# One value product for two heads on 64x64 tiles, and score products with 60 key columns

## The chip, the cores and the metric

The kernel runs on one core of one Trainium2 chip. The metric is the device time of one execution in microseconds. TensorE is called PE here, its weight loads PEld, VectorE DVE, ScalarE ACT, GpSimd POOL and SyncE SP.

## The reference

One layer, on x of shape (2, 128, 256, 256) in float32: halo attention, then a mixture of experts on each pixel, both with a residual. Cut to what matters here:

```
x  = x + conv(layernorm_over_channels(x))
#   conv: qkv = W_qkv x (1x1); windows of 8x8 queries, 12x12 keys and values around them,
#   4 heads of 32 channels; logits = q k / sqrt(32) + relative position (height and width)
#   + a fixed mask that leaves the keys of the query's own parity;
#   softmax, times v, heads joined, W_out
t  = pixels of x as rows of 128 channels
p  = softmax(layernorm(t) @ router_w + router_b)        # 8 experts
t  = t + sum over the two best experts of (weight * (layernorm(t) @ expert_w[e] + expert_b[e]))
```

The mask splits the image into four planes by the parity of row and column; within a plane a window has 4x4 queries and 6x6 keys.

## The kernel before

The image is cut into 64 strips of 8 rows (2 images of 32 strips), each strip into its 4 parity planes: 256 *planes*, each a turn of the main loop over `n` (line 811). A plane has 4 x 128 = 512 queries, that is 16 pairs of windows; the pairs are in two `half`s of 8, counted by `t`. A pair of windows shares `NK` = 6 x 10 = 60 keys; they lie in slots of `SLOT` = 64, so that two halves fill 128 partitions. Keys 60 to 63 of a slot are zero.

On PE a plane has these stages, always in this order:

- `scores`: 16 products of `keys` with `au` (L476), which lay the position terms and the mask into `att[:, :, 0:256]`, one PSUM bank for each head; then 64 products of the keys `kk` with the queries `qs` (L493), one for each `t`, head and half, which add to them. ACT takes the exponential of all into `pT` (L501).
- `project` of the next plane: values `pv` (L349, 4 products), position terms `pu` (L408), keys `pk` (L422), queries `pq` (L447).
- four expert products (L716) of an earlier plane.
- `attend`: 8 products with `ones` (L514), which lay the softmax sums into banks 2 and 3 of `att`, columns 256 to 511; then 64 products of the values `vv` with `pT` (L524), one for each `t`, half and head, into the same columns of banks 0 and 1. DVE transposes the sums (`sT`, L534), takes the reciprocals (`rc`, L536), transposes them back (`rT`, L539) and multiplies (`o`, L544).
- `norms` (L582, 16 products), three expert products (L716), `po` from `o` (L552), one expert product (L716).

DVE makes the other products of the expert part: the gated inputs `xe` of each expert (L707), the sums of the experts (L722), the routing (L615 to L653), and the relative position terms (`uT`, `auT`, `au`: L412 to L396). SP issues nearly all DMAs, in the order of the program. For some of them another engine first writes one element of the tile that is to be loaded, so that the load is placed in time: the copies L688 and L114 on ACT, the memset L690 on DVE.

The order of all engines' instructions is written out by hand in the main loop, under `manual_schedule`; nothing reorders them. From plane 6 on, a plane begins with

```
            if 6 <= n < n_planes:
                nc.tensor.addr_align(BLOCK, offset=BLOCK - FIRST_LIMIT)
```

which puts no-ops into PE's program until the address of the next instruction, counted in instructions, is `BLOCK - FIRST_LIMIT` modulo `BLOCK`. A float32 product is four PE instructions: two times a weight load and a pass.

## Time and profile before

| | us |
|---|---|
| three timed runs | 4332.03, 4342.97, 4343.37 (median 4342.97) |
| the profiled execution | 4328.49 |
| its span, from the first to the last instruction | 4326.7 |

| engine | busy us | share of the span |
|---|---|---|
| PE passes | 4223.3 | 98% |
| PE weight loads | 2472.0 | 57% |
| DVE | 3791.0 | 88% |
| ACT | 1320.7 | 31% |
| POOL | 1087.6 | 25% |

The DMA queue that SP feeds takes 75.9% of the time of the 16 DMA engines; queue q8, which brings PE's program, 1.2%. The granted clock of PE is 0.991 on average.

How to read the lines: a group's line gives line, engine and operation, output <- inputs by the program's names, tile of the array (rows*columns), shapes, and the count; behind the bar the busy time in us and the mean of one in ns; then the idle time of the engine ahead of it, and what ended most of it. "issue" is a wait for nothing that the profile shows. A timeline's line gives start and length in us; consecutive instructions of one kind stand as one, and a length can reach over the next one's start, since the ends of PE's passes are modelled.

### The profile page before, as it was taken

What the parts mean: (1) busy time and instruction counts of PE and PEld (TensorE: products, weight loads), DVE (VectorE), ACT (ScalarE), POOL (GpSimd) and SP (SyncE); (2) the same over time, 40 slices, a digit from 0 to 9 for tenths busy, and PEclk for the clock granted to TensorE, in tenths of its full rate; (3) what the DMA queues carried; (4) which work ended last, traced back from release to release, by engine and by line L of the source; (5) the groups of instructions that cost most, each with busy time, mean ns of one, the idle gap of its engine ahead of it and who ended that gap; (6) DMA issues with size and microseconds to landing.
All of it is one profiled execution on the core that took longest, in us unless ns stands there. A gap on an engine that the chain in (4) does not pass through costs nothing. (4 is left out here: it accounts for less than half of the span.)

```text
span 4326.7 us, 224393 instructions
## 1 busy us (share of the span) xinstructions
PE 4223.3 (98%) x94273; PEld 2472.0 (57%) x94273; DVE 3791.0 (88%) x11850; ACT 1320.7 (31%) x3774; POOL 1087.6 (25%) x1126
## 2 busy tenths in 40 slices
PE   7899999999999999999999999999999999999987
PEld 5455555555555555555555555555555555555553
DVE  5788988988888889988888998898998889899877
ACT  3233332332323232333333233233332333333321
POOL 1222222222222222222222222222222222222211
PEclk8999999999999999999999999999999999999999
DMA  3777778787788778777778778778788787787866
GB/s 109 214 234 247 241 244 244 244 247 235 244 236 242 240 243 248 239 246 239 247 237 247 248 240 247 239 244 250 239 248 244 239 249 237 248 243 244 243 191 193
DMA packets 824578, 1022.17 MB, mean 236 GB/s; under 512 B 137634, under 2 KB 409634, under 8 KB 823594
## 3 DMA queue, kind: packets, MB, share of 16 engines
q1 hardware_dynamic: 822864, 1007.52, 75.9%
q8 instruction: 769, 12.60, 1.2%
q14 instruction: 215, 1.76, 0.1%
q10 hardware_dynamic: 730, 0.29, 0.0%
HBM read 863.78 MB, written 143.75 MB: 233 GB/s over the span
## 5 line engine op out<-in xcount | busy, mean ns | idle before, releaser
L716 PE MATMUL acc<-xe,ew 128*128 128x512 f32 x4096 | 1917.9, 601 | 18.6 <-DVE gb L690 14.3
L716 PEld LDWEIGHTS acc<-xe,ew 128*128 128x128 f32 x4096 | 758.4, 190 | 939.7 <-issue 873.1
L707 DVE TENSOR_TENSOR xe<-xs,gb 128x512 f32<-128x512 f32 x1536 | 950.8, 687 | 11.6 <-DMA gb<-gd 1.5
L711 POOL COPY last<-xe 128x1 f32<-128x1 f32 x256 | 47.6, 186 | 3115.3 <-DVE gb L690 3082.2
L707 POOL TENSOR_TENSOR xe<-xs,gb 128x512 f32<-128x512 f32 x512 | 652.3, 1275 | 1.5 <-PE att L524 1.2
L493 PE MATMUL att<-qs,kcol 32*64 32x32 f32 x32768 | 402.1, 227 | 15.8 <-issue 15.4
L493 PEld LDWEIGHTS att<-qs,kcol 32*64 32x64 f32 x32768 | 397.5, 132 | 19.6 <-issue 18.9
L275 POOL TENSOR_TENSOR xn<-xt,rb 128x512 f32<-128x512 f32 x249 | 374.3, 1503 | 94.6 <-DMA rb<-gd 94.0
L524 PEld LDWEIGHTS att<-pT,vwin 64*32 64x32 f32 x32768 | 349.4, 105 | 42.0 <-issue 4.5
L501 ACT ACTIVATE pT<-att 128x1024 f32<-128x1024 f32 x256 | 262.2, 1024 | 298.8 <-PE att L493 298.8
L524 PE MATMUL att<-pT,vwin 64*32 64x32 f32 x32768 | 346.7, 200 | 2.7 <-issue 1.5
L349 PE MATMUL pv<-wt,xn 128*128 128x128 f32 x2048 | 303.8, 292 | 0.6 <-issue 0.6
L412 DVE STREAM_TRANSPOSE uT<-pu 128x512 f32<-128x512 f32 x256 | 183.6, 717 | 134.9 <-PE pu L408 134.9
L576 ACT ACTIVATE sq<-xt 128x512 f32<-128x512 f32 x505 | 292.6, 630 | 0.0
L396 DVE STREAM_TRANSPOSE au<-auT 128x512 f32<-128x512 f32 x256 | 269.6, 1053 | 9.0
L552 PE MATMUL po<-o,wt 128*128 128x512 f32 x512 | 263.6, 596 | 10.2 <-DVE o L544 6.6
L433 ACT COPY kcol<-pk 128x560 f32<-128x560 f32 (+2 forms) x344 | 183.5, 533 | 275.0 <-PE pk L422 272.2
L408 PE MATMUL pu<-xn,wrel 128*128 128x512 f32 x512 | 267.2, 604 | 0.0
L447 PE MATMUL pq<-xn,wt 128*128 128x512 f32 x512 | 262.1, 592 | 1.7 <-issue 1.7
L422 PE MATMUL pk<-xn,wt 128*128 128x512 f32 (+2 forms) x528 | 261.5, 579 | 0.0
L349 PEld LDWEIGHTS pv<-wt,xn 128*128 128x128 f32 x2048 | 254.1, 195 | 11.5 <-issue 1.0
L476 PEld LDWEIGHTS att<-au,keys 32*64 32x64 f32 x8192 | 117.6, 132 | 228.2 <-PE po L552 183.8
(2437 smaller groups left out, 4856.6 us busy)
## 6 DMA issues: line engine op xcount, KB each, us to landing
gb<-gd SPq DMA_DIRECT2D x2048, 256.0 KB, 5.6
vwin<-vrows SPq DMA_DIRECT2D x512, 240.0 KB, 5.1
xt<-in_x_dram SPq DMA_DIRECT2D x256, 256.0 KB, 6.6
sb<-gd SPq DMA_DIRECT2D x256, 256.0 KB, 4.4
out_dram<-xt SPq DMA_DIRECT2D x256, 256.0 KB, 6.0
rb<-gd SPq DMA_DIRECT2D x249, 256.0 KB, 3.4
vrows<-vr SPq DMA_DIRECT2D x168, 256.0 KB, 3.8
vrows<-vr SPq DMA_DIRECT2D x160, 128.0 KB, 3.6
```

The source lines that it names most:

```text
L275: eng.tensor_tensor(xn[i % 2][:, :, :, k, 1 : PC + 1], ln1_src(i, k).rearrange("p (y j x) -> p y x j", y=2, x=2), rb.rearrange("p (y j x) ...
L349: nc.tensor.matmul(pv[:, j * P : (j + 1) * P], lhsT=xp[:, k, 1 : PC + 1], rhs=wv, start=True, stop=True,)
L396: nc.vector.transpose(au.rearrange("p m a s -> p a s m"), auT[n % 2])
L408: nc.tensor.matmul(pu, lhsT=wrel, rhs=inner, start=True, stop=True)
L447: nc.tensor.matmul(pq, lhsT=wq, rhs=inner, start=True, stop=True)
L493: nc.tensor.matmul(sc[rows, h, 32 * t : 32 * t + 32], lhsT=kk[hp, half * HP + t, :], rhs=qs[hp, m0 : m0 + 2].rearrange("p m a s -> p (m a ...
L501: nc.scalar.activation(pT, att[:, :, 0:HQ], AF.Exp)
L524: nc.tensor.matmul(av[hp, half, 32 * t : 32 * t + 32], lhsT=vv[rows, t, hp], rhs=pT[rows, h, 32 * t : 32 * t + 32], start=True, stop=True,)
L552: nc.tensor.matmul(po, lhsT=wo, rhs=state["o"].rearrange("p f z -> p (f z)"), start=True, stop=True)
L576: nc.scalar.activation(sq, src, AF.Square)
L707: eng.tensor_tensor(self.xe[e], self.xs, self.gb.pop(e), ALU.mult)
L716: nc.tensor.matmul(self.acc, lhsT=ew[:, e, :], rhs=self.xe.pop(e), start=(e == 0), stop=not self.xe)
```

## The change

- The value products: one product takes 64 value channels, those of two heads, and the `pT` of both heads for one `t` and half, 64 columns side by side. It is 64 x 64 on 64 rows: 32 products in place of 64. Half of what it makes is of use (a head's channels with its own `pT`); the other half is left lying. The results fill all 512 columns of banks 0 and 1, where the scores were; `own` is the view of them by `t`, head of the pair `j` and query.
- The softmax sums stay where they were; `av` now names those two banks alone.
- For heads 1 and 3 ACT copies the half of use over the other within PSUM, two copies of 32 partitions, so that `o` can be made by one instruction from `own[:, :, :, 0]`.
- The score products take 60 key columns, not the 64 of a slot, and write 60 partitions.
- The no-ops align a plane to 128 instructions, 88 ahead of a multiple of 128; it was 256, and 99 ahead of a multiple of 256.

```diff
-BLOCK, FIRST_LIMIT = 256, 99
+BLOCK, FIRST_LIMIT = 128, 88
...
-                    rows = slice(half * SLOT, (half + 1) * SLOT)
+                    rows = slice(half * SLOT, half * SLOT + NK)
                     m0 = 2 * (half * HP + t)
                     nc.tensor.matmul(
                         sc[rows, h, 32 * t : 32 * t + 32],
-                        lhsT=kk[hp, half * HP + t, :],
+                        lhsT=kk[hp, half * HP + t, 0:NK],
                         rhs=qs[hp, m0 : m0 + 2].rearrange("p m a s -> p (m a s)"),
...
-        av = att[:, :, HQ:512]
+        av = att[:, 2:4, HQ:512]
+        own = att[:, 0:2].rearrange("p f (t j z) -> p f t j z", j=2, z=32)
...
-                    av[hp, 2 + half], lhsT=ones[rows, :], rhs=pT[rows, h], start=True, stop=True
+                    av[hp, half], lhsT=ones[rows, :], rhs=pT[rows, h], start=True, stop=True
...
-                for h in range(HEADS):
-                    hp = slice(h * DH, (h + 1) * DH)
+                for g in range(2):
+                    gp = slice(2 * g * DH, 2 * (g + 1) * DH)
                     nc.tensor.matmul(
-                        av[hp, half, 32 * t : 32 * t + 32],
-                        lhsT=vv[rows, t, hp],
-                        rhs=pT[rows, h, 32 * t : 32 * t + 32],
+                        att[gp, half, 64 * t : 64 * t + 64],
+                        lhsT=vv[rows, t, gp],
+                        rhs=pT[rows, 2 * g : 2 * g + 2, 32 * t : 32 * t + 32],
...
-        nc.vector.transpose(sT, av[:, 2:4])
+        nc.vector.transpose(sT, av)
         rc = small.tile([P, NQ // 32], F32, tag="rc", name=f"rc{n}")
         nc.vector.reciprocal(rc, sT.rearrange("p f (b k) -> p (f b) k", k=32)[:, :, 0])
+        for h in (1, 3):
+            hp = slice(h * DH, (h + 1) * DH)
+            nc.scalar.copy(own[hp, :, :, 0], own[hp, :, :, 1])
         yield
...
-        nc.vector.tensor_tensor(o, av[:, 0:2], rT, ALU.mult)
+        nc.vector.tensor_tensor(
+            o.rearrange("p f (t z) -> p f t z", z=32),
+            own[:, :, :, 0],
+            rT.rearrange("p f (t z) -> p f t z", z=32),
+            ALU.mult,
+        )
```

## The prediction

> **What bounds the kernel now.** First the page: the busy shares, the costliest groups, the DMA queues.

> ```profile
> PE 4223.3 (98%) x94273; PEld 2472.0 (57%) x94273; DVE 3791.0 (88%) x11850; ACT 1320.7 (31%) x3774; POOL 1087.6 (25%) x1126
> ...
> L493 PE MATMUL att<-qs,kcol 32*64 32x32 f32 x32768 | 402.1, 227 | 15.8 <-issue 15.4
> L493 PEld LDWEIGHTS att<-qs,kcol 32*64 32x64 f32 x32768 | 397.5, 132 | 19.6 <-issue 18.9
> ...
> L524 PEld LDWEIGHTS att<-pT,vwin 64*32 64x32 f32 x32768 | 349.4, 105 | 42.0 <-issue 4.5
> ...
> L524 PE MATMUL att<-pT,vwin 64*32 64x32 f32 x32768 | 346.7, 200 | 2.7 <-issue 1.5
> ...
> q8 instruction: 769, 12.60, 1.2%
> ```

> PE is solid. A product leaves four records (two weight loads, two passes), so a plane has 184 products, 736 PE instructions. With one wait and 31 no-ops (L825) that is 768; queue q8 moved 769 packets of 16,384 bytes, three a plane: one packet holds 256 instructions.

> The timeline of PE next: an undisturbed plane, then three disturbed ones.

> ```profile
> 246.94 0.69 PE L476 MATMUL att<-au,keys 32*64 32x128 f32 x32
> 247.43 1.53 PE L493 MATMUL att<-qs,kcol 32*64 32x32 f32 x128
> 248.88 1.16 PE L349 MATMUL pv<-wt,xn 128*128 128x128 f32 x8
> 249.88 1.02 PE L408 MATMUL pu<-xn,wrel 128*128 128x512 f32 x2
> 250.74 1.02 PE L422 MATMUL pk<-xn,wt 128*128 128x512 f32 x2
> 251.60 1.02 PE L447 MATMUL pq<-xn,wt 128*128 128x512 f32 x2
> 252.46 3.59 PE L716 MATMUL acc<-xe,ew 128*128 128x512 f32 x8
> 255.98 0.66 PE L514 MATMUL att<-pT,ones 64*32 64x256 f32 x16
> 256.44 1.34 PE L524 MATMUL att<-pT,vwin 64*32 64x32 f32 x128
> ```

> ```profile
> 211.33 0.37 PE L493 MATMUL att<-qs,kcol 32*64 32x32 f32 x17
> 213.57 1.22 PE L493 MATMUL att<-qs,kcol 32*64 32x32 f32 x90 [1.87 <-issue]
> ```

> ```profile
> 1088.48 1.45 PE L716 MATMUL acc<-xe,ew 128*128 128x512 f32 x3
> 1090.64 2.31 PE L716 MATMUL acc<-xe,ew 128*128 128x512 f32 x5 [0.71 <-issue]
> ```

> ```profile
> 2674.22 1.15 PE L524 MATMUL att<-pT,vwin 64*32 64x32 f32 x107
> 2675.69 0.32 PE L524 MATMUL att<-pT,vwin 64*32 64x32 f32 x21 [0.31 <-issue]
> ```

> The typical plane repeats in 16.268 us. The breaks stand after 17 score passes, 3 expert passes and 107 value passes: by count, instructions 99, 355 and 611 of the plane, the borders of the 256-instruction blocks, as 256 - 157 = 99 says. Over 239 middle planes the score, value and first expert stages lie 22.4, 6.5 and 6.0 us above their medians: 35 us lost at borders.

> The DMA packet records of queue q8, each with start and duration, say what PE waits for. Wherever PE breaks at a border, it resumes 1.42 us (1.23 to 1.62) after the end of the latest packet, and each border has its own: the packet whose transfer begins some 2.9 us after border 99 was passed is the one border 355 waits for, and so on. So one block is fetched ahead, and passing a border orders the next. In the 197 planes without a score break that packet ends on average 4.62 us after the plane's first product (5th to 95th percentile 3.73 to 5.65); the block is usable at 4.62 + 1.42 = 6.04 us. Border 355 lies at the second expert product, due at 5.52 + 3 x 0.43 = 6.81 us, which mostly hides it.

> **Borders (BLOCK, FIRST_LIMIT).** 32 products fewer are 128 instructions fewer: 608 products' instructions, two waits (a new one stands ahead of L476), 30 no-ops, 640 a plane, 2.5 blocks. Planes alternate: A has borders at 88, 344 and 600, B at 216 and 472. Counting A: the new wait 1, keys to 65, scores to 321, pv to 337, pu to 341, then pk's load, pass, load make 344: the border falls before pk's second pass, due 0.43 us after pk's start at 3.80, so at 4.23 us. The block behind it is ordered at 88, 11 instructions (0.05 us) before today's 99, so usable at 5.99 us. PE stands 5.99 - 4.23 = 1.76 us in every A plane; even the earliest of those packets would be late. pq, the expert products and all behind stand in PE's order behind pk, so nothing takes it back. Of 250 aligned planes half are A; leaving out a few slow last ones, 122 x 1.76 = **+215 us**. The bounds are the packet's 5th and 95th percentile, 0.87 and 2.8 us; a mean over 122 planes moves less, 1.3 to 2.2, or +159 to +268.

> The old breaks go: **-35 us**. What is late next is border 216 of B (ordered at A's 600, during plt) and 88 of A (ordered in B's values); both have 0.4 us more room than today's 99, which cost 22.4 us: **+8**, bounds 0 and +22.

> [...]

> **Values on 64x64.** In steady state L524 starts a product each 16.7 ns, four instructions of 4.17 ns, as L493 does in its fastest stretches; its eight tiles aren't full. Half the products need 0.53 us of issue, but each of four tiles then takes 8 products, 16 passes. A pass costs 0.83 to 0.87 ns a column (428.5 ns for 512, 109 for 128 in L476), so 55 for 64; the load of 64 columns costs some 53 by the difference of the loads (105, 132, 195 ns for 32, 64, 128 columns) and hides behind the pass before if loads overlap passes, as in L349 (111 ns a pass with 128 columns loaded). First load and pass 0.11, 14 x 0.056, stagger 0.02, last pass and turn to plt's shape 0.15: 1.06 us against today's 1.27. The turn from 64x32 to 64x64 is new: other turns cost 0.095 us, and sums to values takes 0.31 instead of 0.17. Net **-0.07 us a plane**. Bounds: -0.2 (no new turn) and +0.75 (each load shows: 14 x 53 ns more).

> [...]

> **Scores with 60 columns.** The load shrinks from 53 to 50 ns behind an issue pace that stays: **0**; bounds -0.09 us a plane (4/64 of 1.456) and +0.05.

> **Copies on ACT, and `o`.** The chain of DVE:

> ```profile
> 2035.24 0.71 DVE L534 STREAM_TRANSPOSE sT<-att 128x512 f32<-128x512 f32 x1
> ...
> 2035.99 0.25 DVE L536 RECIPROCAL rc<-sT 128x16 f32<-128x16 f32 x1
> 2036.28 0.71 DVE L539 STREAM_TRANSPOSE rT<-rc 128x512 f32<-128x512 f32 x1
> 2037.02 0.69 DVE L544 TENSOR_TENSOR o<-att,rT 128x512 f32<-128x512 f32 x1
> ```

> In the built program the first copy waits for sT, the second for the first, `o` for the second. Nearest row L449 (512 columns out of PSUM): 0.59 us; bounds 0.29 (L443) and 1.02 (L501). So 2035.95 + 0.05 + 0.59 + 0.03 + 0.59 + 0.04 = 2037.25: `o` starts 0.25 us late. Behind `o` PE's sequencer waits before po, then works through the no-ops at 73 ns each; the last now ends 0.37 us (median of 239 planes) before the next plane's L476. One no-op fewer (-0.07) and the new wait (+0.13, as the old one took with its gap) make it 0.31 later: just covered by 0.37, less the 0.07 that PE gained. So the PE gain is worth -0.04 a plane, **-10 us**. Were the cover gone, each 0.1 us of copy would cost 25 us; at 1.02 us a copy, +0.8 a plane. ACT rises by 256 x 1.18 = 302 us, under 40%. On ACT the paced copy L114 queues behind the two copies, 6 us later, and with it SP's load of x and the gate row 3 behind it, by some 2 us; x is used planes later, the row over ten us later: nothing.

> **Sum.** Against the profiled execution, 4328.5 us (span 4326.7): + 215 - 35 + 8 - 10 = 4506.5. The three timed runs lie 11 us above it on average (4339.4): about **4517 us**, 4.0% over the median of 4343.

> **Rivals.** *The block is there in time* (faster): two blocks are held ahead, or 88 orders early enough, usable by 4.23 us. Then 4517 - 215 = 4302 us. For it: early packets ended at 3.7 us. Against: 18 planes broke at 355 on the packet ordered at 99, with the same 1.42 us. It decides against me if packets end by 2.8 us after the plane's start.
> *Loads do not hide on 64x64*: 0.75 + 0.07 more in 250 planes, 4517 + 205 = 4722. [...] Against: L349, L476.
> *The copies set the end*: they take 1.02 us; B planes stretch by about 0.8, A planes too since their chain starts with the values: 4717. For it: only 0.06 us of cover is left. Against: L449.

> **Numbers.** The forecast (border wait, 1.3 to 2.2 us) has 0.78, with its own range of 4450 to 4590; unhidden loads 0.06, copies 0.06, block in time 0.10. The range 4430 to 4620 takes in the forecast and smaller forms of the two slow rivals; under 2 in 10 is left out. A difference under about 0.3% can't be told from none by these runs. Faster 0.09, same 0.02, slower 0.89.

> **Signs.** Right: on PE's waits, pk L422 <- issue some 120 times, near 1.6 us each (less than 1.76, since ends are modelled), every second plane 18 us and its neighbours 16.2; q8 near 640 packets; L524's group in 64x64 form at a pace of about 55 ns a pass and tile; no break after 17 score passes. Wrong: PE unbroken at pk, all planes alike, or `o` waited for by po.

## The result, and the profile after

| | before | after |
|---|---|---|
| runs, us | 4332.03, 4338.96, 4342.97, 4343.37 | 4883.63, 4900.64, 4911.19, 4921.99 |
| median of four, us | 4340.97 | 4905.91 |
| profiled execution, us | 4328.49 | 4883.63 |
| granted clock of PE | 0.991 | 0.951 |

The changed kernel is slower: ratio 1.1302, 95% interval 1.1281 to 1.1323. Forecast were 4517 us and at most 4620. The sign held, the size didn't. Below, a time without an interval is that of one execution; those of the kernel before lie between 4312 and 4343 us.

The page of the changed kernel (columns as in the prediction):

```profile
PE 4423.1 (91%) x77889; PEld 2502.5 (51%) x77889; DVE 3804.6 (78%) x11850; ACT 1615.3 (33%) x4286; POOL 1088.9 (22%) x1126
...
PEclk8999999999999999999999999999999999999998
...
q8 instruction: 641, 10.50, 0.9%
...
L493 PE MATMUL att<-qs,kcol 32*60 32x32 f32 x32768 | 426.2, 227 | 244.4 <-issue 244.3
...
L422 PE MATMUL pk<-xn,wt 128*128 128x512 f32 (+2 forms) x528 | 317.0, 651 | 133.1 <-issue 132.9
...
L525 PE MATMUL att<-pT,vwin 64*64 64x64 f32 x16384 | 297.3, 221 | 0.0
```

PE has fewer instructions and is busy for 200 us *more*: L422's mean is 651 ns; in `po`, a product of nearly the same shapes, it is 598. So besides waiting, some products run slower. q8 moved 641 packets, as many as 640 instructions a plane make (256 planes x 640 / 256). The waits of PE (us in total, times, longest):

```profile
PE att L493 <- issue: 244.3, 118, 4.0
PE pk L422 <- issue: 132.9, 115, 2.3
...
PE po L561 <- DVE o L548: 11.3, 5, 2.4
```

The second line was forecast (some 120 times near 1.6 us; measured 115 times 1.16). The first wasn't: every second plane stops in its *scores*, where the kernel before lost 15.4 us in all. The timeline of PE shows both planes of a pair, A first:

```profile
2011.40 0.59 PE L422 MATMUL pk<-xn,wt 128*128 128x512 f32 x1
2012.85 0.59 PE L422 MATMUL pk<-xn,wt 128*128 128x512 f32 x1 [0.85 <-issue]
...
2017.66 0.66 PE L515 MATMUL att<-pT,ones 64*32 64x256 f32 x16
2018.25 1.16 PE L525 MATMUL att<-pT,vwin 64*64 64x64 f32 x64
...
2025.33 0.97 PE L493 MATMUL att<-qs,kcol 32*60 32x32 f32 x75
2027.82 0.75 PE L493 MATMUL att<-qs,kcol 32*60 32x32 f32 x53 [1.52 <-issue]
2028.50 1.26 PE L349 MATMUL pv<-wt,xn 128*128 128x128 f32 x8
2029.56 1.91 PE L408 MATMUL pu<-xn,wrel 128*128 128x512 f32 x2
2031.27 1.81 PE L422 MATMUL pk<-xn,wt 128*128 128x512 f32 x2
```

A breaks at border 344, before pk's second pass. B breaks after 75 score passes, the other border: one wait, 64 instructions of the keys and the next weight load are 66, and with 2 x 75 of the scores 216. Behind that break pu and pk take 1.91 and 1.81 us where 1.02 is normal. The same two planes in windows (window and length, busy us and counts by engine, granted clock, DMA share, GB/s):

```profile
2007.63:2024.85 17.22, 16.37 (x306) 9.17 (x305) 14.78 (x47) 6.17 (x16) 4.68 (x5) 1.00 0.82 232
2024.85:2044.00 19.15, 17.63 (x305) 9.93 (x304) 14.31 (x47) 6.17 (x16) 4.11 (x4) 0.91 0.71 200
```

Plane A has clock 1.00, plane B 0.91: after its break PE was granted half speed for a while. The clock records of the trace put 478.7 us at half speed, in 113 stretches, all but the last one (at the trace's end) 3.413 us long or a multiple of it; before it was 79.8 us, nearly all of it at the start and the end.

Over the 239 middle planes the stages sum up as follows (PE's start times, from one plane's first key product to the next; the mean plane grew from 16.431 to 18.721 us, 547 us in all):

| part | forecast for all planes, us | measured, us |
|---|---|---|
| A: break before pk's second pass (border 344) | +215 | +148 |
| B: break in the scores (border 216) | +8, at most 22 | +275 |
| B: pv, pu and pk at half clock | none | +159 |
| the old breaks | -35 | -39 |
| stages themselves (sums to values +136 ns, values -176, scores -27) | -10 | -16 |

Some 20 us more lie in small breaks of these planes.

### The profile page after: what moved, and what is told of

Same layout as the page of the kernel before. It is cut to its first block, busy times and chain, and to the rows that moved or that the text cites. A ratio compares the mean times of both kernels' runs of the same rounds, so it can differ in the third digit from the quotient of the medians.

```text
span 4881.8 us, 192022 instructions
## 1 busy us (share of the span) xinstructions
PE 4423.1 (91%) x77889; PEld 2502.5 (51%) x77889; DVE 3804.6 (78%) x11850; ACT 1615.3 (33%) x4286; POOL 1088.9 (22%) x1126
## 3 DMA queue, kind: packets, MB, share of 16 engines
q1 hardware_dynamic: 822864, 1007.52, 69.5%
## 4 chain that ended last, share of the span: by engine, by line
PE 89%; issue 8%; DVE 1%; DMA 1%; ACT 0%; SPq 0%; DVEq 0%; ACTq 0%
PE acc L725 36%; PE att L493 8%; PE pv L349 7%; PE pu L408 6%; PE att L525 6%; PE pk L422 6%; PE plt L591 5%; PE pq L447 5%; PE po L561 4%; PE att L476 3%; PE att L515 3%; DMA gb<-gd 0%; ACT att L540 0%; DVE sT L535 0%; DVE o L548 0%
## 5 line engine op out<-in xcount | busy, mean ns | idle before, releaser
L716 DVE TENSOR_TENSOR xe<-xs,gb 128x512 f32<-128x512 f32 x1536 | 951.3, 686 | 18.0 <-PE acc L725 6.0
L716 POOL TENSOR_TENSOR xe<-xs,gb 128x512 f32<-128x512 f32 x512 | 652.2, 1275 | 1.5 <-PE att L525 0.5
L493 PE MATMUL att<-qs,kcol 32*60 32x32 f32 x32768 | 426.2, 227 | 244.4 <-issue 244.3
L540 ACT COPY att<-att 32x512 f32<-32x512 f32 x512 | 283.7, 554 | 1081.6 <-DVE sT L535 1073.6
L493 PEld LDWEIGHTS att<-qs,kcol 32*60 32x60 f32 x32768 | 412.8, 132 | 256.3 <-issue 255.8
L422 PE MATMUL pk<-xn,wt 128*128 128x512 f32 (+2 forms) x528 | 317.0, 651 | 133.1 <-issue 132.9
L501 ACT ACTIVATE pT<-att 128x1024 f32<-128x1024 f32 x256 | 262.2, 1024 | 511.7 <-PE att L493 511.7
L349 PE MATMUL pv<-wt,xn 128*128 128x128 f32 x2048 | 365.3, 333 | 0.9 <-issue 0.9
L408 PE MATMUL pu<-xn,wrel 128*128 128x512 f32 x512 | 337.2, 747 | 4.1 <-issue 4.1
L525 PEld LDWEIGHTS att<-pT,vwin 64*64 64x64 f32 x16384 | 262.2, 134 | 105.4 <-DMA sb<-gd 44.0
L349 PEld LDWEIGHTS pv<-wt,xn 128*128 128x128 f32 x2048 | 307.2, 230 | 12.8 <-issue 1.3
L535 DVE STREAM_TRANSPOSE sT<-att 128x512 f32<-128x512 f32 x256 | 183.0, 715 | 154.7 <-PE att L525 153.6
L525 PE MATMUL att<-pT,vwin 64*64 64x64 f32 x16384 | 297.3, 221 | 0.0
L561 PE MATMUL po<-o,wt 128*128 128x512 f32 x512 | 264.4, 598 | 14.3 <-DVE o L548 11.3
```

The lines of the kernel that those rows point to most:

```text
L349: nc.tensor.matmul(pv[:, j * P : (j + 1) * P], lhsT=xp[:, k, 1 : PC + 1], rhs=wv, start=True, stop=True,)
L408: nc.tensor.matmul(pu, lhsT=wrel, rhs=inner, start=True, stop=True)
L422: nc.tensor.matmul(pk[:, : m * PC], lhsT=wk, rhs=xp[:, part[0] : part[0] + m, 1 : PC + 1], start=True, stop=True,)
L493: nc.tensor.matmul(sc[rows, h, 32 * t : 32 * t + 32], lhsT=kk[hp, half * HP + t, 0:NK], rhs=qs[hp, m0 : m0 + 2].rearrange("p m a s -> p (m ...
L525: nc.tensor.matmul(att[gp, half, 64 * t : 64 * t + 64], lhsT=vv[rows, t, gp], rhs=pT[rows, 2 * g : 2 * g + 2, 32 * t : 32 * t + 32], start ...
L540: nc.scalar.copy(own[hp, :, :, 0], own[hp, :, :, 1])
```

## The experiments

The question is why the block needed at B's border 216 comes so late. One bookkeeping runs through all experiments. The packet that brings a block begins some *lag* after PE has passed the border 256 instructions earlier; it takes about 1.0 us; PE resumes 1.38 us after its end. The *room* is the time from the pass at that border to the pass 256 instructions later, from the starts of PE's passes in undisturbed planes. The break is what is left:

lag + length of the packet + 1.38 - room.

All numbers are medians over the 119 planes of a kind; lags are the start of a record of queue q8, matched by count, minus the start of PE's pass at the border. The expectations divide a stage evenly among its instructions, and so have 3.80, 3.36, 1.48 and 5.1 us of room where the passes have 3.64, 3.47, 1.31 and 5.50.

| kernel, border to need | lag | length | room | break worked out | break measured |
|---|---|---|---|---|---|
| after, 88 to 344 | 2.57 | 0.95 | 3.64 | 1.26 | 1.28 |
| after, 600 to 216 | 3.44 | 0.95 | 3.47 | 2.30 | 2.33 |
| first40, 40 to 296 | 2.09 | 0.97 | 1.31 | 3.13 | 3.21 |
| noops_moved, 600 to 216 | 3.96 | 1.06 | 6.14 | 0.26 | 0.26 |
| noops118, 630 to 246 | 3.18 | 1.01 | 3.64 | 1.93 | 2.03 |
| wait_later, 600 to 216 | 2.42 | 1.00 | 3.47 | 1.33 | 1.36 |
| mid, 600 to 216 | 3.89 | 0.99 | 5.50 | 0.76 | 0.79 |
| half_gates, 600 to 216 | 2.19 | 0.96 | 3.47 | 1.06 | 1.19 |
| few_loads, 600 to 216 | 2.10 | 0.95 | 3.47 | 0.96 | 0.89 |
| few_late_x, 600 to 216 | 1.48 | 0.96 | 3.47 | 0.35 | 0.41 |
| late_x_96, 608 to 224 | 6.45 | 0.99 | 6.07 | 2.75 | 2.76 |

The sum is bookkeeping; what it shows is that PE resumes about the same time after its packet in all these kernels (medians of 1.37 to 1.50 us), and that the break is the rest, to 0.13 us. So a break is settled by two quantities, room and lag. Room follows from the order of the instructions. Lag is the disputed one. It is no pure delay: some packets begin before PE reaches the border (0.6 us before it at the 5th percentile of few_late_x), so the order is given ahead of PE's pass.

**Is it the border, and not the products?** *before88* is the kernel before with the pad alone changed (the no-ops of `addr_align`), *before60* with 60 key columns alone:

```diff
-BLOCK, FIRST_LIMIT = 256, 99
+BLOCK, FIRST_LIMIT = 256, 88      # before88
...
-                    rows = slice(half * SLOT, (half + 1) * SLOT)
+                    rows = slice(half * SLOT, half * SLOT + NK)      # before60
...
-                        lhsT=kk[hp, half * HP + t, :],
+                        lhsT=kk[hp, half * HP + t, 0:NK],
```

> The kernel before with one number changed, FIRST_LIMIT 88 in place of 99 (BLOCK stays 256): borders in every plane at 88, 344 and 600. 344 now lies just ahead of pq, due 4.66 us into the plane; a block ordered at 88 was usable at 5.5 us on average in the changed kernel: a break of 0.8 to 1.3 us at pq in all 250 planes, +200 to +330 us, time 4530 to 4660, at full clock. If borders do not matter in themselves, 4330 to 4345.

> The kernel before with 60 key columns in its score products and nothing else changed: no border moves. If the narrower load and product are what took the score stage of the changed kernel from 1456 to 1429 ns, the same 25 to 30 ns a plane come off here, 6 to 8 us in all: 4319 to 4321 us against the 4326 of its neighbour run. If that came from the stage before it, the score stage stays at 1456 and the time as it is.

before88 took 4554.53 us against 4326.24: every plane is 0.9 us longer around pk and pq (mean period 17.34 instead of 16.43 us), with the old products and a granted clock of 0.991. A border 11 instructions earlier is enough for 5%. One of its planes:

```profile
2000.02 1.02 PE L422 MATMUL pk<-xn,wt 128*128 128x512 f32 x2
2001.96 1.13 PE L447 MATMUL pq<-xn,wt 128*128 128x512 f32 x2 [0.92 <-ACT kcol L433]
```

The profile puts most of these waits down to ACT's copies of the keys, but that isn't their cause: in the kernel before, `pq` starts 0.2 us ahead of the first of these copies (2028.92 and 2029.12 us). Here, too, PE resumes 1.41 us after the end of the packet (1.26 to 1.56 in the planes that break).

before60 took 4332.40 us; its neighbours had 4320.44 to 4330.74. PE's timeline of before60:

```profile
2015.04 1.50 PE L493 MATMUL att<-qs,kcol 32*60 32x32 f32 x128
2016.47 1.16 PE L349 MATMUL pv<-wt,xn 128*128 128x128 f32 x8
```

From L493's start to L349's are 1.43 us, in the kernel before 1.45; by the starts of all passes 1432 and 1456 ns. The narrower product is worth those 24 ns, 6 us in all. The whole doesn't show them: the score breaks came to 29 us in this run, against 22 in the execution of before.

**Where the border lies.** *first99* and *first40* change FIRST_LIMIT of the changed kernel, *noops_moved* and *noops118* put the no-ops ahead of the sums, *no_align* leaves the pad out.

```diff
-BLOCK, FIRST_LIMIT = 128, 88
+BLOCK, FIRST_LIMIT = 128, 99      # first99; first40: 128, 40
...
-            if 6 <= n < n_planes:
-                nc.tensor.addr_align(BLOCK, offset=BLOCK - FIRST_LIMIT)      # removed in no_align too
...
             next(norm, None)
+            if 6 <= n < n_planes:
+                nc.tensor.addr_align(BLOCK, offset=51)      # noops_moved; noops118: offset=21
             next(attn, None)
```

> The changed kernel with FIRST_LIMIT 99 in place of 88: borders in A at 99, 355 and 611 (inside the no-ops), in B at 227 and 483. If the border before pk's second pass was what cost 1.2 us in each A plane, it is gone (355 is due at 6.8 us): -148 us, near 4735. Theories N and W: the block of 227 is still ordered after the no-ops, B keeps 2.2 us and the half clock. Theory Q: as now or better in B, time anywhere between 4400 and 4735.

> The changed kernel with FIRST_LIMIT 40: borders in A at 40, 296 and 552 (in plt, 49 instructions ahead of the wait for o), in B at 168 and 424. In A the block of 296 is ordered 0.3 us into the plane and due 1.8 us into it: a break of 3 to 3.7 us in the scores of A, with the half clock behind it, about 5 us in all. Theory N or W with the order given at the border: the packet of 552 starts before the wait for o ends, B has no break: time 4800 to 4950. If the order needs some 64 instructions more than the border itself, the wait and the no-ops still hold it back: B breaks by 2 us as now, time 5200 to 5400. Theory Q says nothing of this.

> The changed kernel with its 30 no-ops put ahead of the softmax sums (after the four expert products) and not at the end of a plane; planes stay 640 long, borders in A at 88, 344 and, counted without no-ops, 570 (plt), in B at 216 and 442. Theory N (PE's sequencer orders the next block only when it has done the wait for o and the no-ops that follow border 600): that packet now starts well ahead of the next plane, B's break in the scores falls from 2.2 us to under 0.3 us on average, the granted clock is back at 0.99, A keeps its 1.2 us at pk; time 4440 to 4500. Theory W (the wait for o alone holds the order back): the packet starts 1.2 us after that wait ends, about 1 us ahead of the next plane; B's break 0.2 to 0.6 us, time 4480 to 4550. Theory Q (the packet is late because of the other DMA traffic): it still starts some 1.2 us into plane B, time 4860 to 4920.

> The changed kernel with its 30 no-ops ahead of the sums instead of behind the wait for o, and the pad chosen so that the borders lie at 118, 374 and 630 of one plane (374 among the no-ops, 630 where the changed kernel has 600, just ahead of the wait for o) and at 246 and 502 of the other. Theory W (the packet ordered at the last border is held by the wait for o as well): it comes 1.2 to 1.7 us after that wait, about 1 us before the next plane, so the order at 118 is in time and the scores of the other plane, whose border 246 is due 1.35 us in, break by 0.1 to 0.4 us; 4310 to 4400 us at a clock near 0.99. Theory N (only the no-ops hold the packet): no break in either plane, 4290 to 4310 us. The undisturbed plane of the changed kernel being 66 ns under that of the kernel before, no more than 250 x 0.066 + 39 = 55 us of gain can be had.

> The changed kernel without its pads and their no-ops: 610 instructions a plane, so the borders shift by 98 of 256 from plane to plane and every place of the plane is met in turn. If only a border in scores or pk/pq breaks, and by what the order before it was late: about half of the planes with a break of 1 to 2.5 us, some of them followed by half clock; 4450 to 4650 us, that is 2.3 us x 250 less no-ops where nothing breaks. If it is the pad itself that costs (no-ops held behind the wait for o), it is under 4450.

first99 took 4788.40 us, 53 more than expected, since B's break grew: A runs undisturbed (16.205 us), B breaks by 2.9 us after 81 passes. first40 took 4874.07: now B is undisturbed and A breaks after 115 passes, as 66 + 230 = 296 says:

```profile
2000.19 1.34 PE L493 MATMUL att<-qs,kcol 32*60 32x32 f32 x115
2004.45 0.33 PE L493 MATMUL att<-qs,kcol 32*60 32x32 f32 x13 [2.92 <-issue]
```

The break follows the border wherever it is put. noops_moved (4549.88 us) takes the last border of A out of the third expert product into the norms, and B's break falls to 0.26 us in the median, though 11 planes still lose over 2 us. noops118 has the border back just ahead of the wait for `o`, but no no-ops behind it: 4601.3 us (ratio 1.0654, interval 1.0622 to 1.0686), breaks of 2.0 us:

```profile
PE att L493 <- issue: 200.6, 112, 3.5
```

Both theories on record for it, 4400 us at most, failed: the no-ops aren't what holds the packet. no_align, 4622.39 us, met every place in turn and came out within its expectation.

**More room by order.** *wait_later* puts the last expert product ahead of po; *mid* puts pv and pu between the halves of the scores; *mid96* has the order of mid, no-ops ahead of the sums and borders at 96; *mid109* has one more expert product between the halves, the no-ops ahead of the other three, and borders at 109.

```diff
-            next(outp, None)
             ex.product(3)
+            next(outp, None)      # wait_later
...
-            next(score, None)
             next(ahead, None)
+            next(score, None)      # mid, mid96 and mid109; mid109: ex.product(4) ahead of it
```

> The changed kernel with the last expert product of a plane ahead of po in TensorE's order, so that the wait for o stands four instructions further behind border 600, with o long ready when it is reached. Nothing else of the order changes; 600 still lies one instruction before the end of the third expert product, and 256 instructions later the scores are due 3.4 us on. Theory P (place: a border orders the next block when its instruction is executed, the block is usable some 5 us later, and 600 simply lies too late): B breaks after 75 score passes by 2.0 to 2.4 us as before, 4850 to 4920 us. Theory W (the wait for o, one instruction behind the border, holds the order): no wait is left to hold it, the packet comes about 4 us after plt starts, the break falls to 0 to 0.9 us, 4480 to 4600 us.

> The changed kernel with pv and pu of the next plane between the two halves of the score products (two lines of the main loop exchanged). By count the borders stay at 88, 344, 600 and 216, 472, but 1.86 us of large products now lie between the 600 and the 216 that follows: the room from order to need grows from 3.36 to 5.1 us (216 is then the 11th instruction of the second half), while 88 to 344 keeps its 3.80 us. Theory P: B's break falls from 2.2 to 0.1 to 0.5 us and half clock nearly goes, A's break before pk stays at 1.2 us; 4480 to 4560 us. If B's break does not come from that room, the time stays above 4800.

> The kernel mid with the 30 no-ops ahead of the sums and borders at 96, 352, 608 and 224, 480. Rooms from order to need, counted with the stages' undisturbed lengths: 96 to 352 5.49 us, 352 to 608 5.38, 608 to 224 7.78, 224 to 480 6.94, 480 to 96 6.80. Theory P (a block is usable 5.0 us after its border, up to 6 with traffic): no break in the scores, small ones (0.1 to 0.4 us) before the third expert pass and in the norms of A planes, full clock; 4290 to 4370 us, so equal to the kernel before or up to 1% below it. If breaks in the scores stay (over 4450 us), the room is not what counts.

> As mid96, with one expert product more between the score halves (product 4) and the no-ops ahead of the other three, borders at 109, 365, 621 and 237, 493: rooms 5.64, 5.78, 8.10, 6.12 and 6.76 us. Theory P: the smallest room is 0.26 us larger than in mid96, so 20 to 40 us less of breaks: 4270 to 4350 us. Against it: the exponential and the keys come 2.7 and 0.9 us later, which VectorE could turn into waits for o; then 4350 to 4450.

wait_later: 4606.33 us, between its two theories. B's break fell to 1.36 us, with lags from 0.2 to 4.3 us (5th to 95th percentile). Neither theory had foreseen that A's break before pk would fall, too, from 1.28 to some 0.6 us, with the lag behind 88 at 1.74 us:

```profile
PE pk L422 <- issue: 54.0, 83, 1.7
```

mid: 4606.15 us, above its expectation. The added room of 2.03 us brought the break from 2.33 to 0.79, not to 0.1 to 0.5, since the lag rose to 3.89; and splitting the scores costs 0.36 us a plane, which was not foreseen (16.56 us undisturbed, from the turns at both halves, at pu and at pk). mid96: 4422.54 us (1.0238, 1.0218 to 1.0259), outside its 4290 to 4370. Its border 608 has 8.1 us of room, over twice that of the changed kernel, and still 57 of 119 planes broke by 1.3 us: the lag there is below 1.4 us in a quarter of the planes and over 7.0 in another. mid109: 4528.12 us (1.0484, 1.0466 to 1.0501), worse than mid96, and outside its expectation. The undisturbed plane grew again, to 16.85 us, and a new break came, where mid96 lost 0.6 us:

```profile
PE acc L725 <- issue: 103.3, 127, 6.5
```

Border 365 lies among the no-ops ahead of the three expert products, and PE resumes only 2.94 us after the end of its packet, where it is 1.38 elsewhere. The no-ops left behind the border, 18 of 71 ns, would make up 1.3 us of it (an estimate). Room helps where the lag keeps still, and it doesn't.

**The traffic.** *half_gates* loads four gate rows a plane instead of eight, *one_gate* one, and both use them for the other experts; *few_loads* also leaves out the value windows, so none of these computes the layer; *few_first99* is few_loads with FIRST_LIMIT 99; *few_late_x* issues the load of x and the store in the next plane.

```diff
         def fetch(self, e, eng):
+            if e:                  # half_gates: if e % 2:
+                return
...
         def take_values(n):
+            if n > 7:              # few_loads, few_first99, few_late_x
+                return
...
+            if n:                  # few_late_x, behind next(ahead) of the next turn
+                load_x((n + 8) // 4, (n + 8) % 4, paced=True)
+            while to_store:
+                store(*to_store.pop())
...
-            load_x((n + 9) // 4, (n + 9) % 4, paced=True)
...
-            while to_store:
-                store(*to_store.pop())
```

> The changed kernel with only the gate rows of the even experts loaded (four of eight transfers a plane) and used for the odd ones too, which leaves out part of the loads and changes the values. Theory D (packets ordered while TensorE runs take 2.6 to 3.0 us because other transfers fill the queues): with the gate rows halved the lag after 88 falls towards 1.3, the 1.24 us break before pk/pq falls under 0.3, the scores break less too; below 4750 us. Theory E (the lag follows from where the order stands in TensorE's own stream): lag 2.57, breaks 1.24 and 2.2 us as before, 4850 to 4920 us.

> The changed kernel with one gate row of eight loaded a plane and used for all experts, which leaves out seven of eight of those loads and changes the values. Theory D (a packet of TensorE's program waits behind the transfers that SP has under way; with none it begins 1.15 us after its border, as it does now where PE has been blocked for long): lags near 1.2 to 1.8 us at all borders, the break of A before pk (room 3.80 us, need 1.15 + 1.0 + 1.38) mostly gone, that of B (room 3.36) 0.2 to 0.8 us; 4310 to 4450 us. Theory P (a fixed lag of 2.4 us behind the execution of the border): A 0.9 us, B 1.3 us as with half the rows; 4560 to 4610 us. Theory W (the wait for o holds the order of 600): A 0.2, B stays at 2 us; over 4600 us.

> As one_gate, and without the loads of the value windows from plane 8 on, which leaves out those too: two of ten large loads behind the attention remain. Theory D: lags 1.1 to 1.3 us throughout, A without a break, B 0.1 to 0.3 us, 4300 to 4340 us, that is the kernel before less its own breaks. Theory P: as one_gate, 4560 to 4610.

> As few_loads, with the borders of the kernel FIRST_LIMIT 99: 611 lies behind the wait for o among the no-ops, 1.4 us before the scores are due. Theory D with the place of the border: even with no traffic 1.15 + 1.0 + 1.38 = 3.5 us are needed, so B breaks after 81 passes by 2.0 to 2.3 us and half clock follows in some planes; 4560 to 4680 us. If traffic alone made the breaks, none is left: 4300 us.

> As few_loads, with the two transfers that SP still issues just ahead of the wait for o (the load of x and the store of the output) issued in the next plane instead, after its pv; order of all engines' computing unchanged. In few_loads the transfers under way between the wait for o and 2.4 us after it are those two, and the packet of border 600 begins 2.47 us after that wait, when they have ended, whether the border is 600 or (few_first99) 611. Theory D (the packet stands behind transfers issued before it): without them it begins about 0.95 us after border 600 is executed, that is 1.3 us after the wait for o and 1.3 us before the next plane, usable 1.0 us into it, before the scores need it at 1.3: no break left in either plane, 4265 to 4300 us. Theory W (held by the wait for o and the no-ops behind it): still 2.5 us after the wait, break of 0.9 us in B, 4375 to 4390 us.

| kernel | us | share of q1 | lag behind 88 | lag behind 600 | break of A | break of B |
|---|---|---|---|---|---|---|
| after | 4905.91 | 69.5% | 2.57 | 3.44 | 1.28 | 2.33 |
| half_gates | 4593.64 | 57.6% | 2.41 | 2.19 | 1.06 | 1.19 |
| one_gate | 4391.78 | 44.7% | 0.96 | 2.14 | 0 | 0.93 |
| few_loads | 4386.65 | 31.8% | 0.95 | 2.10 | 0 | 0.89 |
| few_late_x | 4310.44 | 33.2% | 0.97 | 1.48 | 0 | 0.41 |

None of these touches the order of PE's products, yet the time falls by 595 us, and the last is 15 us under its neighbour run of the kernel before (4325.20). The waits of PE in few_loads, then in few_late_x:

```profile
PE att L495 <- issue: 83.8, 118, 1.3
```

```profile
PE att L495 <- issue: 26.5, 77, 0.8
```

L495 is the score product there (two lines were added above it). No line for pk is left in either: A's break before pk is gone. The theory of traffic (D) got the direction right and the sizes only in part: half_gates was to bring A's break under 0.3 us, and it stayed at 1.06, while B's halved; few_loads was to end at 4340 us at most, few_late_x at 4300 with no break left. The fixed lag (P) and the wait for `o` (W) missed by more. few_first99 took 4387.53 us. I had expected 4560 to 4680 from its bad place, or 4300; instead its packet begins 2.52 us after the wait for `o`, in few_loads 2.47, though its border, 611, lies eleven instructions behind 600, beyond the wait and `po`. Something else set that moment, and few_late_x shows a part of it: with the two transfers out of the way the packet begins 1.86 us after that wait. Theory W, that the wait itself holds it, wanted 2.5; theory D wanted 1.3.

**With all loads.** *before_late_x* and *late_x_96* move the same two transfers with everything else loaded, in the kernel before and in the changed one with no-ops ahead of the sums (offset 43).

> The kernel before with the load of x and the store of the output issued in the next plane, after its pv, and nothing else changed. Theory D: the packet ordered at border 611 of the values (lag 2.6 us, up to 4.6) no longer stands behind those two transfers, the score breaks after 17 passes (22 us in all) shrink to under 10, and the time falls by 10 to 25 us, 4300 to 4318 beside 4325. Against it: the two transfers then meet other packets or loads, and the breaks at the expert products (6 us) grow; then 4320 to 4345.

> The changed kernel, all its loads kept, with what the runs point to: no-ops ahead of the sums, borders at 96, 352, 608 and 224, 480 (rooms 5.49, 5.38, 6.04, 8.69 and 6.80 us where the changed kernel has 3.80 and 3.36) and the load of x and the store in the next plane. Theory D with rooms: lags of 2.0 to 3.0 us need 4.4 to 5.4 us, so no break in most planes; 4290 to 4340 us, that is equal to the kernel before or up to 0.8% below it. If the lag stays at 3 to 4 us as in the kernel with moved no-ops, B breaks in half its planes by 1 us: 4400 to 4460.

Both failed: 4427.73 us (1.0244, 1.0222 to 1.0266) and 4714.66 (1.0892, 1.0864 to 1.092). The waits of PE in before_late_x, then in late_x_96:

```profile
PE att L524 <- issue: 104.6, 133, 1.9
```

```profile
PE att L493 <- issue: 273.3, 107, 4.7
```

In before_late_x the score breaks did go (2.2 us in all, from 22.4). But the two transfers now stand before the next packet: the lag behind border 355 rose from 0.69 to 1.74 us, and the values break at 611 in 157 of 239 planes. In late_x_96 the lag behind 608, in the norms, is 6.45 us. No version I ran is faster than the kernel before with all of the work done.

## Why the prediction was right or wrong

**The border before pk** was right in place and count, and smaller: 148 us in the middle planes for 215. The mis-sized term is the lag: 2.57 us behind 88, where 2.9 had been taken over from 99. one_gate, in which A doesn't break, says what the rest of it is: with little traffic the lag is 0.96 us, the block is there 0.2 us before pk needs it, and the rival "block in time" would have been right.

**"What is late next is border 216 of B (ordered at A's 600, during plt) ... +8"** is the step that failed. First the place. By the count of the prediction itself the norms are instructions 526 to 589 and the three expert products behind them 590 to 601: border 600 falls just ahead of the last pass of the third expert product, not in plt. From there to 216 are 3.47 us; from 611 to 99 of the kernel before they are 6.48. So B hadn't "0.4 us more room than today's 99" but 3 us less. With the prediction's own 2.9 us of lag that would have been 2.9 + 1.0 + 1.42 - 3.47 = 1.85 us in 120 planes, +222 instead of +8; measured were 2.33 us and +275. Second the lag, 3.44 behind 600; half_gates brought it to 2.19 and half the break away.

**The clock** was in no term: 159 us. It follows from the breaks in B: few_late_x, with breaks of 0.4 us, has 53.6 us at half speed in the whole execution, before 79.8. With 222 and 159 in the sum the forecast would have been 4517 - 8 + 222 + 159 = 4890. That this is near 4906 is in part luck: in it A's 215 is 67 us too large and B's 222 is 53 too small.

**Values on 64x64** were right: the stage takes 1.092 us (forecast 1.06; before 1.268), the sums 592 ns with the new turn (forecast +0.14, measured +0.136). The loads hide; the rival of unhidden loads is out. (Its price counted 0.07 us twice: 14 x 53 ns over the forecast are 0.74 us a plane, 186 us, not 205.) **Scores with 60 columns**: -24 to -27 ns against 0, inside the bounds. **Copies**: 554 ns each (forecast 0.59), and PE waited for `o` five times, 11.3 us, as the waits show; the rival of the copies is out. The old breaks went as said.

**Signs.** A planes 17.58 us on average (forecast 18), their neighbours 19.85 (16.2). The second was named as a sign of being right, and it failed; q8's 641 packets, the pace of the values (58 ns a pass and tile for 55) and the end of the breaks after 17 score passes came as named.

What stays open is the lag itself. That transfers of SP delay the packets is shown: less traffic shortens the lags, and moving two transfers moves the delay from one packet to another. Which transfer delays which packet by how much is not: behind a border in the norms the median lag was 2.43 us in first40 (border 552), 3.96 in noops_moved, 5.9 with two humps in mid96 and 6.45 in late_x_96, and the number of SP's transfers under way at the border, on average 2.6, 2.7, 2.1 and 1.7, doesn't put these in order. The lags are also counted from PE's pass, while the records of the sequencer's own instructions are ahead of it: the wait for `o` comes 0.37 us before the pass at border 600, the first no-op of noops118 over 5 us before the sums. How much of a lag is the sequencer's is open. Whether the wait for `o` has a part of its own where all loads run is open too.

## What to carry to other kernels

Where the program streams in blocks (of 256 instructions here), list every border with the instruction it falls on, and for each the time from there to the instruction a block later, in undisturbed stage lengths. The smallest of these rooms are the first to look at (3.47 and 3.64 us here; the score stage alone takes 256 instructions in 1.43 us), but a wide one is no safety by itself: mid96 broke at 8.1. Test a change of instruction count by moving the pad alone in the old kernel, as before88 does. And the program's packets came later here with more data under way (lag behind 88: 0.96 us with SP's queue at 45%, 2.57 at 70%): a load that nobody waits for can still stop an engine, by delaying its instructions.
